# The first expert layer of a four-layer decoder: rows turned two tiles ahead, its weights on another queue, a small summary moved, and additions fixed behind their gathers

## The chip, the cores and the metric

The kernel runs on one core of a Trainium2 chip, as one program launched once. The metric is the device time of that core in microseconds (us), from the program's start to its end. Lower is better. The engines are named as in the profile: PE does matrix products, PEld is the loading of its weights (the operand that stays put), DVE is the vector engine, ACT the scalar engine (ScalarE), POOL is GpSimd, and SP issues most of the DMA transfers.

## The reference

Four decoder layers are applied to `x` (4 batches, 256 rows, 256 columns) with a context `ctx` (4, 1601, 256), all in fp32. Each layer is `x + attention(x, ctx)` and then `x + ffn(norm(x))`. Only parts of layers 0 to 2 matter here.

The feed-forward part of layer 0 is a mixture of 32 experts, of which each of the 1024 rows takes 8:

```
sel_w, sel_e = top_k(x @ gate_w.T, 8);  sel_w = softmax(sel_w)
g, u = x @ w_gate_proj[e].T, x @ w_up_proj[e].T          # I = 96
out = sum over the 8 chosen e of sel_w[e] * (silu(g) * u) @ w_down_proj[e].T
```

The attention of layer 1 reads the context through a decayed scan and then takes the mean of all its states, so that one vector per batch, the summary, is added to every row before a LayerNorm:

```
s[t] = K * s[t-1] + (ctx[t] @ W_in.T + b_in);  summary = mean over t of (s[t] @ W_out.T + b_out)
y = x + summary;  x = x + layernorm(y) * gamma + beta
```

The feed-forward part of layer 1 is a mixture of 8 experts with 2 chosen per row, and shared experts beside them. Layer 2 is attention with 4 key and value heads of 128 columns; its keys are normalised products of the context, `rms_norm(ctx @ wk_ctx)`, and its values are `ctx @ wv_ctx`. They depend on nothing that layers 0 and 1 compute.

## The kernel before, in words

**Layer 0's experts** (`l0_ffn`, from line 311) don't multiply every row by every expert. The 1024 x 8 pairs of row and expert are sorted by expert into NS = 95 tiles of 128 rows, each of a single expert. Eight DMAs, issued by SP (L338, L339), bring the weights, eight experts in each. `normed` (L105) normalises x, writes it to DRAM as `xd` from ScalarE's queue (L113) and turns it for the product with the router, whose logits are copied at L356. A long chain of small DVE steps (L356 to L378) finds the eight largest logits of each row and the place of each pair in the sorted order. To find the source row of each place, one-hot matrices are built by DVE (`cols` and `rows`, L385 to L389, of four groups of 128 rows at a time) and multiplied by PE (L397). The result is copied to `src`.

Then comes the loop of 95 tiles. POOL gathers 128 rows of `xd` by indirect DMA (L405, four buffers `f0xr`). `brought` turns them on PE (L444) and ScalarE copies the turned rows out of PSUM into `f0xsT` (L446, three buffers). `through` multiplies them by the gate and up weights of the tile's expert, which a register picks (`f0gu`), and ScalarE and DVE form silu(g) * u (L456, L457). `turned` turns that (L462, L464), `down` multiplies it by the down weights, DVE copies the result (L471) and SP writes it to `yd` in DRAM. The steps are staggered: in step s the order is `through(s)`, `brought(s + 1)`, `turned(s - 1)`, `down(s - 2)`.

**Adding back** (`l0_add`, L490). For each of 8 groups of 128 rows, POOL gathers eight results per row from `yd` (eight indirect DMAs, 64 in all). One group later DVE adds them with their gates to x (L510). Every second group, `l1_xattn` does the attention of layer 1 for one batch on DVE. When t is 1 the function `l1_summary` (L1115) computes the four summaries: two small products of `csum` with W_in (`mean`, L1125), four of the mean with W_out (`sm`, L1132). Its weights and vectors are loaded by `l1_open` (L1100). The loads of layer 1's expert weights (`l1_weights`, L630: eight DMAs) are issued from SP, one at each step of t.

**Layer 1's experts** (`l1_ffn`, L643) work in the same way with 23 tiles. Its tail (L836 to L847) gathers two results per row for eight groups and adds each right after the statement that gathers it.

**What fills PE.** `fill(n)` (L98) takes n steps of `l2_early` (L1147), which prepares layer 2's keys and values for 15 pairs of batch and head. One pair takes 7 product steps (8 passes of 256 columns, two ScalarE copies to `kr_early` and `va_early`, L1177 and L1178, and a write of the values by SP, L1179; `va_early` has four buffers), a norm, and 4 turning steps (L1202, a ScalarE copy, L1204, and a write, L1205). The list F0 says how many steps go where in the routing of layer 0 (8 after the logits, 10 in `slots`, 8 before each half of the one-hot products, 4 before the loop), G0 = 9 how many follow each group of `l0_add`, and F1 those of layer 1. What is left is done in layer 2's attention. The context of the next batch (`ctxT`) is loaded when a batch's first pair begins.

**What sets the order.** The program is written in the order of the work, and a planner in the framework orders each engine's instructions from it: among those that are ready by its own estimates, the one that stands earlier in the program goes first. `pin` (L96) forces an instruction to stay behind the one that was traced before it on the same engine. Each engine then works strictly through its list, and an instruction that waits holds all behind it. DMAs of SP and ScalarE wait in these lists too.

Of the kernel before, what the change touches and what calls it, by code (L numbers as in the profile page):

```python
# [11 lines left out]
F32 = mybir.dt.float32  # L12
BF16 = mybir.dt.bfloat16
U8 = mybir.dt.uint8
F16 = mybir.dt.float16
# [3 lines left out]
ALU = mybir.AluOpType  # L19
# [5 lines left out]
B = 4  # L25
# [20 lines left out]
F0 = [0, 0, 0, 0, 8, 10, 8, 4]  # L46
G0 = 9
REGS = 4
F1 = [1, 2, 2, 3, 0, 24]
# [8 lines left out]
class Kernel:  # L58
# [254 lines left out]
    def l0_ffn(self, one):  # L313
# [17 lines left out]
        with ExitStack() as es:  # L331
            wp = es.enter_context(tc.tile_pool(name="f0w", bufs=1))
            rt = es.enter_context(tc.tile_pool(name="f0r", bufs=1))
            two = es.enter_context(tc.tile_pool(name="f0two", bufs=2))
            w13 = wp.tile([P, E0, 2, 2 * I0], F32, name="f0w13")
            w2 = wp.tile([I0, E0, D], F32, name="f0w2")
            for e in range(0, E0, 8):
                nc.sync.dma_start(w13[:, e : e + 8], self.i["l0_w13"][:, e : e + 8])  # L338
                nc.sync.dma_start(w2[:, e : e + 8], self.i["l0_w2"][:, e : e + 8])  # L339
# [14 lines left out]
            self.fill(F0[B])  # L354
            l = rt.tile([P, 8, E0], F32, name="l0_l")
# [45 lines left out]
            nc.vector.tensor_copy(src, st[:, :NS])  # L401
            xr = []
# [38 lines left out]
            def brought(n):  # L441
                tp = ps.tile([P, 2, P], F32, name="f0tpx", tag="tp")
                for k in range(2):
                    nc.tensor.transpose(tp[:, k, :], xr[n][:, k * P : (k + 1) * P], self.ident)  # L444
                t = two.tile([P, 2, P], F32, name="f0xsT", bufs=3)
                nc.scalar.copy(t, tp)  # L446
# [183 lines left out]
    def l1_weights(self, pool):  # L630

        w = self.w1f = []
        for n, shape, parts in (
            ("l1_s13", [P, 2, 2, 2 * I1], 1), ("l1_s2", [P, 3, D], 1), ("l1_w13", [P, E1, 2, 2 * I1], 4),
            ("l1_w2", [H1, E1, 2, D], 2),
        ):
            w.append(pool.tile(shape, F32, name=n))
            c = shape[1] // parts
            for e in range(0, shape[1], c):
                self.pin(self.nc.sync.dma_start(w[-1][:, e : e + c], self.i[n][:, e : e + c]))  # L640
                yield

    def l1_ffn(self):  # L643
# [11 lines left out]
        with ExitStack() as es:  # L655
# [3 lines left out]
            s13, s2, w13, w2 = self.w1f  # L659
            xd = self.dram.tile([NT, D], F32, name="f1xd")  # L660
# [176 lines left out]
            for t in range(8):  # L837
                for r in range(K1):
                    yt = two.tile([P, D], F32, name="f1yt", bufs=6)
# [4 lines left out]
                    xt = self.x[t // 2][:, t % 2, :]  # L844
                    nc.vector.scalar_tensor_tensor(xt, yt, gate[:, r, t : t + 1], xt, ALU.mult, ALU.add)
                self.fill(F1[B + 1] // 8)
# [253 lines left out]
    def l1_open(self, es):  # L1100
        nc, i = self.nc, self.i
        one = self.a1 = es.enter_context(self.tc.tile_pool(name="a1", bufs=1))
# [5 lines left out]
        nc.sync.dma_start(b_in, i["l1_bin"].rearrange("(k p) -> p k", p=P))  # L1108
        rows = self.rows1 = {}
        for n in ("l1_bout", "l1_gamma", "l1_beta"):  # L1110
            rows[n] = one.tile([P, D], F32, name=n)
            nc.sync.dma_start(rows[n], i[n].to_broadcast([P, D]))
        self.w1 = (*w, b_in)

    def l1_summary(self):  # L1115

        nc, one = self.nc, self.a1
        w_in, w_out, b_in = self.w1
        nc.vector.tensor_scalar(b_in, b_in, self.swb, None, ALU.mult)
        mean = one.tile([P, 2, B], F32, name="mean")  # L1120
# [5 lines left out]
        self.summary = []  # L1126
        for b in range(B):
# [3 lines left out]
            sm = one.tile([P, D], F32, name=f"sm1{b}")  # L1131
            nc.vector.tensor_tensor(sm, sp, self.rows1["l1_bout"], ALU.add)  # L1132
            self.summary.append(sm)
# [12 lines left out]
    def l2_early(self, ctxT):  # L1146
# [17 lines left out]
        def products(u):  # L1164
# [3 lines left out]
            for m in range(0, NM, 2):  # L1168
# [7 lines left out]
                va = e2.tile([P, 2, HD2], F32, name="va_early", bufs=4)  # L1176
# [857 lines left out]
    def run(self):  # L2034
# [7 lines left out]
        with ExitStack() as es1:  # L2042
# [4 lines left out]
            one = es1.enter_context(tc.tile_pool(name="f0one", bufs=1))  # L2047
            self.l0_ffn(one)
            weights = self.l1_weights(es1.enter_context(tc.tile_pool(name="f1w", bufs=1)))
            with ExitStack() as es:  # L2050
                self.l1_open(es)
                self.l0_add(self.a1, weights)
            self.l1_ffn()
# [136 lines left out]
```

## Time and profile before

| | us |
|---|---|
| three runs | 2672.34, 2672.18, 2665.82 |
| median | 2672.18 |
| the profiled execution's own time | 2689.12 |
| span in its profile | 2687.4 |
| busy in the span: PE, PEld | 2503.5, 1507.0 |
| busy in the span: DVE, ACT, POOL | 1464.8, 1315.8, 751.5 |
| layer 0's attention ends | 141 |
| routing of layer 0 | 141 to 226 |
| loop of 95 tiles | 231 to 398 |
| `l0_add` | 398 to 524 |
| routing of layer 1, its loop, its tail | 524 to 612, to 670, to 702 |

A row of "costliest groups" names the line, engine, operation and tiles, the busy time and the mean of one in ns, and then the idle time of the engine just before it with what ended it. "PE MATMUL fill" at L74 are the products of `l2_early`, since L74 is the line of the helper that issues all products. In the answer on waits, a line gives the engine, the instruction that waited and what for, the total in us, how often, and the longest. In an answer in order of time, the first column is the start in us, the second the length, and `x4` that four instructions of one kind are put together. The 40 slices are 67.2 us each.

### The profile page before, as it was taken

To read this page: it belongs to the slowest core of one execution; us is meant where nothing else is said; L and a number is where in the kernel's file an instruction comes from. 1 tells how busy PE (TensorE), PEld (TensorE's weight loads), DVE (VectorE), ACT (ScalarE), POOL (GpSimd) and SP (SyncE) were. 2 spreads that over 40 slices of the span, in tenths; PEclk is the share of its full clock that TensorE was granted. 3 is DMA by queue.
4 is the path that set the end of the run, shared out by engine and by line. 5 is a ranking of instruction groups with operands and counts; after the bars stand their busy time and mean duration, and the time that the engine had idled before them with its cause. 6 is when DMAs were issued, how large, how long until landed. Compare 5 with 4: busy or idle time off the path is not lost. (4 is left out here: it accounts for less than half of the span.)

```text
span 2687.4 us, 47127 instructions
## 1 busy us (share of the span) xinstructions
PE 2503.5 (93%) x17800; PEld 1507.0 (56%) x17816; DVE 1464.8 (55%) x3031; ACT 1315.8 (49%) x2959; POOL 751.5 (28%) x1038
## 2 busy tenths in 40 slices
PE   7979994899689999999999999998998999999997
PEld 4667773677545555555555555655554554545553
DVE  6343534743467777777777777675234314233323
ACT  2334442452454445444444444442325775757775
POOL 1014546202334433433444444332101102001000
PEclk8989997899899999999999999999999999999998
DMA  5154575633621111111111110003212100000000
GB/s 199 57 194 137 161 149 155 210 98 89 196 95 45 41 38 46 45 46 45 45 45 45 45 43 28 9 9 133 90 72 73 33 2 27 4 3 2 5 6 5
DMA packets 93631, 186.24 MB, mean 69 GB/s; under 512 B 14924, under 2 KB 62736, under 8 KB 91312
## 3 DMA queue, kind: packets, MB, share of 16 engines
q1 hardware_dynamic: 79142, 150.80, 16.7%
q0 software_dynamic: 10416, 28.46, 4.7%
q10 hardware_dynamic: 3850, 3.97, 0.5%
q8 instruction: 145, 2.38, 0.4%
q14 instruction: 78, 0.64, 0.1%
HBM read 136.77 MB, written 46.42 MB: 68 GB/s over the span
## 5 line engine op out<-in xcount | busy, mean ns | idle before, releaser
L1448 ACT ACTIVATE p<-s,nm 128x448 f32<-128x448 f32 (+1 forms) x512 | 326.5, 644 | 424.3 <-DVE nm L1444 263.7
L1909 ACT ACTIVATE e<-s 128x1024 f32<-128x1024 f32 (+1 forms) x448 | 404.3, 960 | 158.7 <-PE s L74 153.9
L74 PE MATMUL s<-kT,qT 128*32 128x448 f32 (+1 forms) x4096 | 470.2, 556 | 10.0 <-ACT p L1448 5.0
L74 PE MATMUL o<-pT,va 128*128 128x256 f32 (+2 forms) x1920 | 431.1, 376 | 6.0 <-DVE pT L1490 6.0
L1484 POOL TENSOR_SCALAR p<-p,rm 128x448 f32<-128x448 f32 (+1 forms) x512 | 322.5, 652 | 370.0 <-DVE rm L1477 339.7
L74 PEld LDWEIGHTS o<-pT,va 128*128 128x128 f32 (+1 forms) x1920 | 344.4, 191 | 93.1 <-issue 51.4
L1490 DVE STREAM_TRANSPOSE pT<-p 128x896 f32<-128x896 f32 (+1 forms) x256 | 283.9, 1128 | 36.7 <-POOL p L1484 33.1
L1444 DVE TENSOR_REDUCE nm<-s 128x2 f32<-128x896 f32 (+1 forms) x256 | 282.7, 1105 | 3.4
L74 PE MATMUL s<-qb,kT 32*128 32x256 f32 (+1 forms) x3328 | 267.9, 404 | 13.2 <-ACT e L1909 11.0
L74 PEld LDWEIGHTS s<-kT,qT 128*32 128x32 f32 x4096 | 123.6, 109 | 264.9 <-issue 222.5
L74 PE MATMUL o<-e,va 128*32 128x256 f32 (+1 forms) x3328 | 235.7, 391 | 1.3 <-DVE os L2006 1.3
L74 PEld LDWEIGHTS s<-qb,kT 32*128 32x128 f32 (+1 forms) x3328 | 162.9, 181 | 105.2 <-issue 75.4
L74 PE MATMUL fill<-wkc_early,ctxT 128*128 128x256 f32 x780 | 184.6, 396 | 30.4 <-ACT va_early L1178 19.3
L74 PEld LDWEIGHTS fill<-wkc_early,ctxT 128*128 128x128 f32 x780 | 151.5, 197 | 59.6 <-ACT va_early L1178 21.9
L74 PEld LDWEIGHTS o<-e,va 128*32 128x32 f32 (+1 forms) x3328 | 90.6, 110 | 114.9 <-issue 74.9
L1936 POOL TENSOR_TENSOR x<-x,t 128x32 f32<-128x32 f32 x64 | 14.7, 250 | 438.7 <-DVE t L1931 438.7
L1441 DVE TENSOR_TENSOR s<-s,mask 128x128 f32<-128x128 f32 (+1 forms) x256 | 83.2, 325 | 67.3 <-PE s L74 62.3
L405 POOL DMA_INDIRECT f0xr<-f0xd,f0src x95 | 90.8, 956 | 80.6 <-PE f0tph L462 64.6
L1336 POOL TENSOR_TENSOR qo<-qo,qt 128x512 f32<-128x512 f32 x32 | 40.7, 1272 | 242.0 <-DVE rm L1477 139.6
L1448 ACT ACTIVATION_READ_ACCUMULATOR p<-s,nm 128x1 f32 x512 | 101.8, 199 | 0.0
L74 PE MATMUL f0gu<-f0w,f0xsT 128*128 x380 | 87.4, 353 | 1.4 <-ACT f0xsT L446 1.2
L1177 ACT COPY kr_early<-fill 128x256 f32<-128x256 f32 (+1 forms) x105 | 37.4, 356 | 101.3 <-PE fill L74 90.6
(510 smaller groups left out, 3494.2 us busy)
## 6 DMA issues: line engine op xcount, KB each, us to landing
ctxT<-in_ctxT SPq DMA_DIRECT2D x10, 1664.0 KB
f0yd<-f0ys SPq DMA_DIRECT2D x95, 128.0 KB
vd<-va_early SPq DMA_DIRECT2D x90, 128.0 KB
kd<-kT_early SPq DMA_DIRECT2D x45, 256.0 KB
kT<-kd SPq DMA_DIRECT2D x15, 768.0 KB
va<-vd SPq DMA_DIRECT2D x15, 768.0 KB
wq<-in_l_wq SPq DMA_DIRECT2D x16, 512.0 KB
wo<-in_l_wo SPq DMA_DIRECT2D x16, 512.0 KB
```

Of the source, the lines that this page charges most:

```text
L74: self.nc.tensor.matmul(out, lhsT, rhs, start=start, stop=stop, **kw)
L405: nc.gpsimd.indirect_dma_start(out=t, out_offset=None, in_=xd[:, :], in_offset=bass.IndirectOffsetOnAxis(ap=src[:, n : n + 1], axis=0),)
L1177: nc.scalar.copy(kr[:rows, m : m + n, :], tp[:rows, :n, :HD2])
L1336: nc.gpsimd.tensor_tensor(o1, o1, t2, ALU.add)
L1441: nc.vector.tensor_tensor(sv, sv, mask[:, 2 * c : 2 * c + 2, : nt - CT, :].rearrange("p n t i -> p n (t i)"), ALU.add)
L1444: nc.vector.tensor_reduce(nm[:, 2 * c : 2 * c + 2], s[:, :, : nt * 32], AX.X, ALU.max, negate=True)
L1448: nc.scalar.activation(p[:, n, : nt * 32], s[:, n, : nt * 32], AF.Exp, bias=nm[:, e : e + 1], accum_out=sm[:, e : e + 1],)
L1484: nc.gpsimd.tensor_scalar(p[:, n, : nt * 32], p[:, n, : nt * 32], r[:, e : e + 1], 1.0, ALU.mult, ALU.mult)
L1490: nc.vector.transpose(pT[:, 2 * c : 2 * c + 2, :nt, :].rearrange("p n t i -> p n (t i)"), p[:, :, : nt * 32])
L1909: nc.scalar.activation(e[:kr, :, :n, :], s[t][:kr, :, :n, :], AF.Exp, scale=1.0 / math.sqrt(HD3))
L1936: nc.gpsimd.tensor_tensor(xt, xt, t[:, q], ALU.add)
```

## The change

The change does the following.

1. The weights of layer 0's experts are issued by ScalarE in 16 DMAs of four experts each, instead of by SP in eight of eight experts.
2. F0 is 6, 8, 4, 4 instead of 8, 10, 8, 4. The one-hots are built in four parts of two groups, not two of four, so that 4 fill steps stand before each of four parts. They have a pool of their own, closed before the loop's buffers are opened.
3. `l1_summary` is called in `l0_ffn`, after the logits and the fill that follows them. Its loads (`l1_load`) are issued before `l0_ffn` starts; gamma and beta stay in `l1_open`.
4. Rows are brought two tiles ahead of their products: `brought(0)` and `brought(1)` stand ahead of the loop, and step s calls `brought(s + 2)`. `f0xsT` has four buffers.
5. In `l0_add` the additions are pinned, so that DVE keeps them in the order of the program. The loads of layer 1's expert weights begin at t = 6, so that three are issued there; the other five are issued at the start of `l1_ffn`.
6. In layer 1's tail the additions are done two groups after their gathers and are pinned; `f1yt` has `3 * K1` buffers, the same six. Three fill steps follow each of ten passes (30) instead of each of eight (24).
7. `va_early` has six buffers instead of four.

The core of the diff:

```diff
-F0 = [0, 0, 0, 0, 8, 10, 8, 4]
+F0 = [0, 0, 0, 0, 6, 8, 4, 4]
-F1 = [1, 2, 2, 3, 0, 24]
+F1 = [1, 2, 2, 3]
+G1 = 3
...
-            for e in range(0, E0, 8):
-                nc.sync.dma_start(w13[:, e : e + 8], self.i["l0_w13"][:, e : e + 8])
-                nc.sync.dma_start(w2[:, e : e + 8], self.i["l0_w2"][:, e : e + 8])
+            for e in range(0, E0, 4):
+                nc.scalar.dma_start(w13[:, e : e + 4], self.i["l0_w13"][:, e : e + 4])
+                nc.scalar.dma_start(w2[:, e : e + 4], self.i["l0_w2"][:, e : e + 4])
...
             self.fill(F0[B])
+            self.l1_summary()
...
-            for half in range(2):
+            hot = es.enter_context(ExitStack())
+            oh2 = hot.enter_context(tc.tile_pool(name="f0oh", bufs=2))
+            for part in range(4):
                 ones = []
-                for t in range(4 * half, 4 * half + 4):
-                    cols = two.tile([P, NS, K0], F16, name="f0cols", bufs=4)
-                    rows = two.tile([P, P, K0], F16, name="f0rows", bufs=4)
+                for t in range(2 * part, 2 * part + 2):
+                    cols = oh2.tile([P, NS, K0], F16, name="f0cols")
+                    rows = oh2.tile([P, P, K0], F16, name="f0rows")
...
-                t = two.tile([P, 2, P], F32, name="f0xsT", bufs=3)
+                t = two.tile([P, 2, P], F32, name="f0xsT", bufs=4)
...
             brought(0)
+            brought(1)
             for s in range(NS + 2):
                 if s < NS:
                     hs[s] = through(s)
-                    if s + 1 < NS:
-                        brought(s + 1)
+                    if s + 2 < NS:
+                        brought(s + 2)
...
-            if t == 1:
-                self.l1_summary()
             if t:
                 xt = self.x[(t - 1) // 2][:, (t - 1) % 2, :]
                 for r in range(K0):
-                    nc.vector.scalar_tensor_tensor(xt, rows.pop(0), gate[:, t - 1, r : r + 1], xt, ALU.mult, ALU.add)
+                    self.pin(
+                        nc.vector.scalar_tensor_tensor(xt, rows.pop(0), gate[:, t - 1, r : r + 1], xt, ALU.mult, ALU.add)
+                    )
...
             self.fill(G0)
-            next(weights, None)
+            if t > 5:
+                next(weights, None)
...
+            for _ in weights:
+                pass
...
-            for t in range(8):
-                for r in range(K1):
-                    yt = two.tile([P, D], F32, name="f1yt", bufs=6)
+            rows = []
+            for t in range(10):
+                for r in range(K1 if t < 8 else 0):
+                    yt = two.tile([P, D], F32, name="f1yt", bufs=3 * K1)
...
+                    rows.append(yt)
+                if t > 1:
+                    xt = self.x[(t - 2) // 2][:, (t - 2) % 2, :]
+                    for r in range(K1):
+                        self.pin(
+                            nc.vector.scalar_tensor_tensor(
+                                xt, rows.pop(0), gate[:, r, t - 2 : t - 1], xt, ALU.mult, ALU.add
+                            )
+                        )
-                self.fill(F1[B + 1] // 8)
+                self.fill(G1)
...
-                va = e2.tile([P, 2, HD2], F32, name="va_early", bufs=4)
+                va = e2.tile([P, 2, HD2], F32, name="va_early", bufs=6)
...
+            self.l1_load(one)
             self.l0_ffn(one)
```

More of the change, by code (lines that the diff above doesn't have):

```diff
@@ L333, in l0_ffn @@
             rt = es.enter_context(tc.tile_pool(name="f0r", bufs=1))
-            two = es.enter_context(tc.tile_pool(name="f0two", bufs=2))
             w13 = wp.tile([P, E0, 2, 2 * I0], F32, name="f0w13")
             w2 = wp.tile([I0, E0, D], F32, name="f0w2")
-            for e in range(0, E0, 8):
-                nc.sync.dma_start(w13[:, e : e + 8], self.i["l0_w13"][:, e : e + 8])
-                nc.sync.dma_start(w2[:, e : e + 8], self.i["l0_w2"][:, e : e + 8])
+            for e in range(0, E0, 4):
+                nc.scalar.dma_start(w13[:, e : e + 4], self.i["l0_w13"][:, e : e + 4])
+                nc.scalar.dma_start(w2[:, e : e + 4], self.i["l0_w2"][:, e : e + 4])
             src = rt.tile([P, NS], U32, name="f0src")
@@ L401, in l0_ffn @@
             nc.vector.tensor_copy(src, st[:, :NS])
+            hot.close()
+            two = es.enter_context(tc.tile_pool(name="f0two", bufs=2))
             xr = []
@@ L630, in l1_weights, with l1_ffn @@
     def l1_weights(self, pool):
-        w = self.w1f = []
-        for n, shape, parts in (
+        sizes = (
             ("l1_s13", [P, 2, 2, 2 * I1], 1), ("l1_s2", [P, 3, D], 1), ("l1_w13", [P, E1, 2, 2 * I1], 4),
             ("l1_w2", [H1, E1, 2, D], 2),
-        ):
-            w.append(pool.tile(shape, F32, name=n))
+        )
+        self.w1f = [pool.tile(shape, F32, name=n) for n, shape, _ in sizes]
+        yield
+        for w, (n, shape, parts) in zip(self.w1f, sizes):
             c = shape[1] // parts
             for e in range(0, shape[1], c):
-                self.pin(self.nc.sync.dma_start(w[-1][:, e : e + c], self.i[n][:, e : e + c]))
+                self.pin(self.nc.sync.dma_start(w[:, e : e + c], self.i[n][:, e : e + c]))
                 yield
-    def l1_ffn(self):
+    def l1_ffn(self, weights):
         nc, tc = self.nc, self.tc
@@ L843, in l1_ffn @@
                     )
-                    xt = self.x[t // 2][:, t % 2, :]
-                    nc.vector.scalar_tensor_tensor(xt, yt, gate[:, r, t : t + 1], xt, ALU.mult, ALU.add)
-                self.fill(F1[B + 1] // 8)
+                    rows.append(yt)
[6 more added lines that the diff above has]
+                            )
+                        )
+                self.fill(G1)
             self.scaler = nc.gpsimd
@@ L1097, in l2_add, with l1_load @@
             )
-    def l1_open(self, es):
+    def l1_load(self, one):
         nc, i = self.nc, self.i
-        one = self.a1 = es.enter_context(self.tc.tile_pool(name="a1", bufs=1))
         w = []
@@ L1108, in l1_open @@
         nc.sync.dma_start(b_in, i["l1_bin"].rearrange("(k p) -> p k", p=P))
+        b_out = one.tile([P, D], F32, name="b_out")
+        nc.sync.dma_start(b_out, i["l1_bout"].to_broadcast([P, D]))
+        self.w1 = (*w, b_in, b_out)
+        self.summary = [one.tile([P, D], F32, name=f"sm1{b}") for b in range(B)]
+        self.mean1 = one.tile([P, 2, B], F32, name="mean")
+    def l1_open(self, es):
+        nc, i = self.nc, self.i
+        one = self.a1 = es.enter_context(self.tc.tile_pool(name="a1", bufs=1))
         rows = self.rows1 = {}
-        for n in ("l1_bout", "l1_gamma", "l1_beta"):
+        for n in ("l1_gamma", "l1_beta"):
             rows[n] = one.tile([P, D], F32, name=n)
             nc.sync.dma_start(rows[n], i[n].to_broadcast([P, D]))
-        self.w1 = (*w, b_in)
     def l1_summary(self):
-        nc, one = self.nc, self.a1
-        w_in, w_out, b_in = self.w1
+        nc = self.nc
+        w_in, w_out, b_in, b_out = self.w1
         nc.vector.tensor_scalar(b_in, b_in, self.swb, None, ALU.mult)
-        mean = one.tile([P, 2, B], F32, name="mean")
+        mean = self.mean1
         for h in range(2):
@@ L1125, in l1_summary @@
             nc.vector.tensor_scalar(mean[:, h, :], ms, b_in[:, h : h + 1], 1.0 / M, ALU.add, ALU.mult)
-        self.summary = []
         for b in range(B):
@@ L1130, in l1_summary @@
                 self.mm(sp, mean[:, h, b : b + 1].to_broadcast([P, P]), w_out[:, h, :], h == 0, h == 1)
-            sm = one.tile([P, D], F32, name=f"sm1{b}")
-            nc.vector.tensor_tensor(sm, sp, self.rows1["l1_bout"], ALU.add)
-            self.summary.append(sm)
+            nc.vector.tensor_tensor(self.summary[b], sp, b_out, ALU.add)
     def l1_xattn(self, b):
@@ L2047, in run @@
             one = es1.enter_context(tc.tile_pool(name="f0one", bufs=1))
+            self.l1_load(one)
             self.l0_ffn(one)
             weights = self.l1_weights(es1.enter_context(tc.tile_pool(name="f1w", bufs=1)))
+            next(weights)
             with ExitStack() as es:
@@ L2052, in run @@
                 self.l0_add(self.a1, weights)
-            self.l1_ffn()
+            self.l1_ffn(weights)
         self.l2_xattn()
```

## The prediction

> **What bounds the kernel now.** I read the 40 slices first, then the busy time by stretches, then the waits and the order of time inside the stretches that are not full.
>
> ```profile
> PE   7979994899689999999999999998998999999997
> PEclk8989997899899999999999999999999999999998
> 135.00:160.00 25.00, 22.48 (x128) 19.92 (x127) 11.44 (x49) 7.98 (x18) 2.65 (x10) 1.00 0.75 253
> 160.00:200.00 40.00, 24.46 (x109) 20.34 (x110) 15.24 (x46) 16.36 (x40) 6.99 (x9) 0.79 0.52 165
> 200.00:250.00 50.00, 44.36 (x221) 35.97 (x220) 16.61 (x34) 20.05 (x57) 20.18 (x21) 0.90 0.40 128
> 250.00:400.00 150.00, 149.39 (x804) 111.97 (x803) 68.31 (x202) 69.87 (x266) 79.26 (x84) 1.00 0.65 155
> 400.00:450.00 50.00, 22.17 (x84) 15.98 (x83) 14.63 (x37) 9.55 (x23) 30.42 (x33) 0.66 0.49 148
> 450.00:524.00 74.00, 57.27 (x244) 45.38 (x242) 55.20 (x148) 32.55 (x90) 34.07 (x36) 0.88 0.63 199
> 524.00:612.00 88.00, 85.95 (x440) 68.62 (x439) 39.07 (x145) 47.21 (x121) 10.40 (x28) 1.00 0.37 114
> ```
>
> A row of the second kind is a stretch, its length, then busy time (and count) of PE, PEld, DVE, ACT and POOL, the granted clock, the DMA share, GB/s. From about 700 us on PE is full and the change touches nothing there. It acts between 141 and 702 us, where PE is lacking in two places: 160 to 200 (15.5 us idle) and 400 to 524 (44.6 us). PE is the bound elsewhere. In 250 to 400, the loop of 95 sorted tiles, PE looks full, yet its weight side waits:
>
> ```profile
> PEld f0gu L74 <- ACT f0xsT L446: 31.8, 85, 0.4
> 301.53 0.62 PEld L74 LDWEIGHTS f0gu<-f0w,f0xsT 128*128 128x128 f32 x4 [0.38 <-ACT f0xsT L446]
> 303.18 0.62 PEld L74 LDWEIGHTS f0gu<-f0w,f0xsT 128*128 128x128 f32 x4 [0.38 <-ACT f0xsT L446]
> L405 POOL DMA_INDIRECT f0xr<-f0xd,f0src x95 | 90.8, 956 | 80.6 <-PE f0tph L462 64.6
> ```
>
> One tile takes 303.18 - 301.53 = 1.65 us, and in it the first weight load stands 0.38 us for ScalarE's copy of the turned rows. POOL, with 0.956 us a gather, is idle half of the time. The first hole comes from writes:
>
> ```profile
> PE fill L74 <- ACT va_early L1178: 17.1, 1, 17.1
> SPq L1179 <- DMA f0xd<-xn: 12.0, 1, 12.0
> SPq L339 <- DMA f0w<-in_l_w: 3.3, 1, 3.3
> ```
>
> PE stands 17.1 us for a copy to a value tile (va_early) whose four buffers are all waiting to be written out; SP holds those writes behind the eight weight loads. The second hole, in order of time:
>
> ```profile
> 412.11 1.16 PE L74 MATMUL fill<-csum,l_win 128*128 128x4 f32 x8 [2.89 <-ACT va_early L1178]
> 421.05 1.22 PE L74 MATMUL fill<-l_wout,mean 128*128 128x256 f32 x2 [7.78 <-issue]
> 434.96 2.07 PE L74 MATMUL fill<-l_wout,mean 128*128 128x256 f32 x4 [7.80 <-issue]
> 443.39 2.07 PE L74 MATMUL fill<-l_wout,mean 128*128 128x256 f32 x4 [6.35 <-DVE sm L1132]
> ```
>
> These few matmuls of the mean summary are some 9 us of work spread over 409 to 445 us while POOL gathers; fills queue behind them.
>
> **What the Trainium skill says.** "DMA: Bandwidth & Descriptors", section "Issuing engines are not separate DMA queues": loads issued by another engine run on the same 16 DMA engines and save sequencer time only. The trace agrees that the transfer is the limit: the 9.4 MB of weights, landing in 146 to 171, keep the share at 0.93 to 1.00 and move 293 to 349 GB/s. The same page, "Queues, rings and completion order": SP's and ScalarE's queues are separate rows which each engine serves in turn. So the value writes need no longer follow all weights; no run here shows both rows loaded. "TensorE: Matmul & The Clock Gate", section "What's actually happening": an idle PE is granted half the clock. The trace agrees: 0.54 in 410 to 447 us.
>
> **The change, part by part**, against the profiled execution (2689.1 us, span 2687.4). That one lies 16.9 us above the median 2672.2 of the three runs; I carry differences over unchanged.
>
> *Weights by ScalarE (141 to 200).* Bytes are the same, 9.4 MB or about 30 us at 310 GB/s. Issues go from 8 to 16; SP's rows took 0.34 to 0.55 us each, so ScalarE spends 16 x 0.42 = 6.7 us issuing. Good side: value writes bypass the weights, and six buffers instead of four hold two products' time more, so the 17.1 us go. Bad side: in before SP's last weight issue already waited 3.3 us for an earlier weight load. If every issue past the eighth waits likewise, ScalarE stands until eight of 16 loads have landed, some 4.7 MB at 310 GB/s = 15 us. Queued behind it are the xnT copies, ln_rs and the fills' copies; PE and the routing chain wait for those. Then PE's hole only moves from 157 to 142. Gain: 0 to 17; I take 6.
>
> *Fill steps.* F0 goes from 8+10+2x8+4 = 38 to 6+8+4x4+4 = 34. A unit of 11 steps is about 12.9 us of PE, 1.17 a step: 4.7 us gained here. Four parts of one-hots (2 x 1.65 us on DVE from the rows 0.55, 0.69, 0.41 us) hide beneath their 4 steps = 4.7 us; without this cover, 3.3 us each for the last two parts. The 4 steps reappear later; G0 stays 81, the tail of layer 1 gets 30 for 24, and layer 2 is left with 2 fewer: 2.3 us gained. The six extra in the tail cost nothing if PE is idle there (612 to 701: 71.8 of 89 busy), 7 us if not. I take 0.
>
> *Summary in the routing chain.* 24 small matmuls and 7 DVE steps, about 5 us of PE work and 2.5 of DVE. DVE's routing steps end at 171.5 and their product is first wanted by PE at 203.2, so DVE has some 30 us to spare. I take +3, bounds 0 and +31 (if hand-offs are as slow here as in 412 to 443). Four moved loads (0.5 MB) cost 2 us of DMA, before the routing starts.
>
> *ctxT load.* It is issued at 230.2 now, 1.66 MB, while the first gathers run; 231 to 240 us shows PE 3.4 of 9 us busy at a DMA share of 0.95. With four steps fewer the load falls past the loop. Up to 5 us gained, some given back at the gathers after it: I take 2.
>
> *Rows two tiles ahead.* The copy is then done a tile early, so the 0.38 us wait goes. Not all of it counts: PE's array is still busy with the down product during part of it. By the starts of its passes a tile without a wait is 4 x 0.163 (gate/up) + 2 x 0.11 + 0.107 (turns) + 2 x 0.215 (down) = 1.41 us, 0.25 less than 1.65. Next limits: POOL at 0.956 plus 0.30 between gathers = 1.26; ScalarE 0.25 + 0.37 + 0.26 = 0.88; DVE 0.67; DMA share 0.65 x 1.65/1.41 = 0.76. None reaches 1.41, POOL comes near. 95 x 0.25 = 24 us gained; bounds 13 and 34 (0.14 and 0.36 a tile).
>
> *l0_add (398 to 524).* The summary leaves, so fills stay in PE's stream during the first gathers; five of the eight weight loads of layer 1 leave too and three come late. POOL's 64 gathers need 64 x 1.26 = 81 us and took 97.3 (402.6 to 499.9). 81 fill steps are 95 us of PE; only 49 were through at 524, the rest ran in the routing of layer 1. The floor is 44.6 us of PE idle removed. But part of that hole belongs to the gathers' tail (a fill's transposes wait for ScalarE copies 6 to 7 us late at 462 to 475 too), and nothing in the change makes that faster. Pinned additions stand in DVE's order ahead of the fills' scales and the next norm: if a gather is late, these are late as well, and PE's fills behind them. Gain 0 to 45; I take 20.
>
> *Layer-1 weights.* Five of eight loads, 5 x 704 KB = 3.5 MB or 12 us at 300 GB/s, are now issued together at the start of l1_ffn, ahead of the fills' writes on SP. They land before the loop at 612. Fills may stall like those at 157, less what six buffers hold: 0 to 12 us; I take +4.
>
> *Tail of layer 1.* 16 gathers x 1.25 = 20 us pace it as before; additions two tiles late add nothing. 0, bounds -5 and +5.
>
> Sum: -6 - 4.7 - 2.3 + 3 - 2 - 24 - 20 + 4 + 0 = -52 us. Profiled 2637; median 2672 - 52 = 2620, 1.9% faster.
>
> **The rivals.**
> *The loop finds another limit*: the planner keeps the turns where they were, or POOL's gathers and the random 1 KB rows set the pace near 1.6 us. For: 1.26 us is only 0.15 below 1.41, and copies of down products already waited 12.4 us for write-outs near the loop's end. Against: POOL's idle time of 80.6 us. The loop then gains 5: 2620 + 19 = 2639.
> *l0_add keeps its time*: the late hand-offs come from gathering itself and pinned additions repeat them. For: 462 to 475. Against: fills at 402 to 409 run at full speed beside gathers. 2620 + 20 = 2640.
> *Everything goes well*: stall 17, l0_add 40, loop 26 gained, nothing lost at layer 1 or to the summary: another 40 us, 2580.
> *Slower*: ScalarE is held by its own weight issues for the whole transfer. With value writes taking half of the DMA, 9.4 MB at 150 GB/s is 63 us. From the end of this hold on the chain needs 8.7 us (turn, copy, logits: 141.4 to 150.1), 21.4 (DVE), 22.7 (203.2 to 225.9, first to last one-hot product) and 5 (gather, first turn): 58 us, so the loop starts at 141 + 63 + 58 = 262, not 231: +31. A hold of 32 us starts the loop where it starts now. With the loop's 13 at the low end, nothing from l0_add, 4 lost at layer 1 and 2 gained in layer 2: 31 - 13 + 4 - 2 = +20: 2692. It decides from a hold of 32 + 11 = 43 us. Against it: only the first eight of the sixteen loads must have landed before the last is issued.
>
> **How the numbers follow.** Forecast 0.44, 2605 to 2632; loop limit 0.15; l0_add unchanged 0.20; all well 0.12; slower 0.09. A measurement tells 0.3%, 8 us, from no change. Faster: 0.44 + 0.12 + 0.20 + 0.15, less 0.05 for two of these rivals together with the small costs at their high ends: 0.86; same 0.05; slower 0.09. The range leaves out the slower rival and about half of the good one: 2583 to 2667.
>
> **What would show it.** Right: the f0xsT wait gone and gate/up loads 1.4 us apart; no fill wait on va_early of over 5 us near 157; no summary lines after 400; PE over 80% busy in l0_add. Wrong: ScalarE's DMA issues with waits between 142 and 158 and xnT copies behind them; summary lines stretched over 30 us in the routing; a tile still at 1.6 us; PE idle beside the gathers as now; fills waiting on va_early after l1_ffn's start.

## The result, and the profile after

The changed kernel takes 2637.6 us (median of 4 runs, 2635.6 to 2638.5) against 2669.9 for the kernel before (4 runs, 2665.8 to 2672.3). The ratio is 0.9879, with a 95% interval of 0.9862 to 0.9897: 32 us or 1.2% less. The forecast was 2620, 52 us less, in a band of 2605 to 2632 that 2637.6 overshoots. The changed kernel's profiled execution took 2638.45 us with a span of 2636.7, so between the two *profiles* the span fell by 50.7 us. The difference between 50.7 and 32 is the first thing to explain: the profiled execution of before, from which every term was taken, was 17 us slower than the other runs of before, while that of after is not.

The rows of the changed kernel that answer to those of before. First the 40 slices, then busy time by stretches (length; PE, PEld, DVE, ACT, POOL; clock; DMA share; GB/s):

```profile
PE   7989988898799999999999999998998999999997
PEclk8989999999999999999999999998999999999998
```

```profile
135.00:160.00 25.00, 13.32 (x73) 11.79 (x71) 4.07 (x13) 3.27 (x8) 2.66 (x10) 0.78 0.78 265
160.00:200.00 40.00, 38.85 (x171) 31.88 (x172) 25.91 (x87) 16.88 (x41) 6.37 (x7) 0.84 0.43 148
250.00:400.00 150.00, 140.12 (x817) 123.15 (x816) 73.25 (x210) 72.31 (x271) 90.21 (x107) 0.98 0.75 181
400.00:450.00 50.00, 43.95 (x205) 35.15 (x204) 36.59 (x82) 27.72 (x75) 34.01 (x38) 0.97 0.66 197
450.00:524.00 74.00, 62.36 (x289) 50.14 (x287) 51.67 (x131) 35.43 (x95) 18.25 (x20) 0.93 0.71 230
```

The hole of 160 to 200 is closed, but one has opened in 135 to 160. In 400 to 450 PE is busy for 44 us where it was 22. The loop, in order of time on the weight side:

```profile
302.26 0.73 PEld L75 LDWEIGHTS f0gu<-f0w,f0xsT 128*128 128x128 f32 x4
303.67 0.73 PEld L75 LDWEIGHTS f0gu<-f0w,f0xsT 128*128 128x128 f32 x4
```

No wait stands behind these rows any more, and a tile takes 303.67 - 302.26 = 1.41 us. POOL is idle before its gathers (now L410) for 51.3 us instead of 80.6.

```profile
L410 POOL DMA_INDIRECT f0xr<-f0xd,f0src x95 | 92.3, 972 | 51.3 <-PE f0tph L467 43.2
```

The longest wait of PE in 141 to 231 us, and then the only rows of the mean summary. They now stand in the routing of layer 0, within 5.5 us, with four short products of the routing between the first row and the second and no idle time:

```profile
PE f0gu L75 <- ACT xnT L72: 11.7, 1, 11.7
```

```profile
173.48 0.51 PE L75 MATMUL fill<-csum,l_win 128*128 128x4 f32 x4
174.79 0.51 PE L75 MATMUL fill<-csum,l_win 128*128 128x4 f32 x4
175.15 3.87 PE L75 MATMUL fill<-l_wout,mean 128*128 128x256 f32 x16
```

To see where the time went, the span is cut at five events that every kernel has, read from the views in order of time: the first gate/up product of the loop, the last down product, the first and last products of layer 1's loop, and the last product of a fill with the context (called the last fill; it falls in layer 2's attention). Lengths in us:

| | before, first profile | before, second | changed | changed, again |
|---|---|---|---|---|
| start to the loop | 232.8 | 233.1 | 231.0 | 233.0 |
| loop of 95 tiles | 164.8 | 165.0 | 146.2 | 146.8 |
| its end to layer 1's loop (l0_add, routing) | 214.9 | 200.2 | 188.8 | 189.0 |
| layer 1's loop | 57.6 | 57.7 | 57.7 | 57.6 |
| its end to the last fill (tail and start of layer 2) | 63.5 | 54.6 | 55.1 | 54.2 |
| rest | 1953.8 | 1955.5 | 1957.9 | 1959.0 |
| span | 2687.4 | 2666.1 | 2636.7 | 2639.6 |

The second profile of before and the repeat of the changed kernel are experiments told below. Up to the last fill, 31.8 us separate the second column from the third: 2.1 before the loop, 18.8 in it, 11.4 behind it, and 0.5 lost in the tail. The rest is 2.4 us longer, which is less than its spread over the profiles of before (1953.8 to 1960.2, with a third one below).

### The profile page after: what moved, and what is told of

It is laid out like the page before. It is cut to its first block, busy times and chain, and to the rows that moved or that the text cites. A ratio compares the mean times of both kernels' runs of the same rounds, so it can differ in the third digit from the quotient of the medians.

```text
span 2636.7 us, 47077 instructions
## 1 busy us (share of the span) xinstructions
PE 2491.9 (95%) x17816; PEld 1517.6 (58%) x17816; DVE 1480.0 (56%) x3039; ACT 1310.9 (50%) x2957; POOL 750.8 (28%) x1030
## 5 line engine op out<-in xcount | busy, mean ns | idle before, releaser
L1959 POOL TENSOR_TENSOR x<-x,t 128x32 f32<-128x32 f32 x64 | 14.7, 252 | 439.7 <-DVE t L1954 439.7
L410 POOL DMA_INDIRECT f0xr<-f0xd,f0src x95 | 92.3, 972 | 51.3 <-PE f0tph L467 43.2
L75 PE MATMUL f2gu<-f2wgu,f2xsT 128*128 x176 | 84.3, 603 | 0.6 <-ACT f2xsT L72 0.3
```

Source lines behind the costliest of these rows:

```text
L75: self.nc.tensor.matmul(out, lhsT, rhs, start=start, stop=stop, **kw)
L410: nc.gpsimd.indirect_dma_start(out=t, out_offset=None, in_=xd[:, :], in_offset=bass.IndirectOffsetOnAxis(ap=src[:, n : n + 1], axis=0),)
L1959: nc.gpsimd.tensor_tensor(xt, xt, t[:, q], ALU.add)
```

## The experiments

After the result my theory was: the loop and the emptier l0_add are real gains, ScalarE's queue has moved the first hole and not removed it, and some 17 us of the holes in the first profile are not typical. The rival: the profile of before is right, and the changed kernel has a cost that its profile doesn't show.

The runs stood in three sets of four, each set on one chip and each timed beside the kernel before there: 2670.1, 2694.4 and 2672.9 us. On the second set's chip this kernel was slower, so the four runs there are compared with each other, by stretches, and not with those of the other sets.

**Before, once more** (no edit).

> The kernel before, unchanged, profiled once more. Theory A (the profiled execution of before was not typical: it took 2689 us where the other runs took 2666 to 2672, and the surplus sits in the hole beside the gathers, 400 to 450 us): this profile's own time is 2665 to 2675, PE's busy time in 400 to 450 us is 32 or more instead of 22, and the matmuls of the mean summary lie closer together than 412 to 445. Theory B (profiling always slows this kernel, or the surplus is spread over the whole span): own time near 2689 again, the hole as before, or the difference in no single stretch.

Measured: ratio 0.9998 (0.9988 to 1.0008), profiled span 2666.1. The summary's rows in this profile:

```profile
412.90 1.55 PE L74 MATMUL fill<-csum,l_win 128*128 128x4 f32 x8 [3.17 <-ACT va_early L1178]
422.75 5.77 PE L74 MATMUL fill<-l_wout,mean 128*128 128x256 f32 x16 [8.30 <-DVE mean L1125]
```

In the first profile the sixteen products with W_out came in groups of 2, 6, 4 and 4 with gaps of up to 8 us, from 421 to 445; here they run in one piece, after one gap of 8.3. PE's busy time in 400 to 450 is 33.5 us instead of 22.2. The table shows where the first profile was longer: 14.7 us behind the loop, 8.9 in layer 1's tail, nowhere else. In both, POOL gathers while PE's fills come in short bursts. Theory A holds, though 8.9 us of the surplus lie in the tail, which it had not named.

**Two tiles ahead alone.** Before, with the fourth `f0xsT` buffer, the one-hots in four parts so that the buffers fit, and

```diff
+            brought(1)
...
-                    if s + 1 < NS:
-                        brought(s + 1)
+                    if s + 2 < NS:
+                        brought(s + 2)
```

> Before with the rows turned two tiles ahead and the fourth f0xsT buffer alone; the one-hots get the pool of their own in four parts, since the buffers don't fit otherwise, and the number of fill steps stays 38. Theory A (the loop alone gives what its stretch of the changed kernel shows, 18 to 19 us, and nothing later takes it back, since PE bounds what follows): 2669 - 18 = 2651, ratio 0.993. Rival (the results of the loop only reach the gathers of l0_add earlier, which write-outs of the last tiles hold back, so that part is lost): 2660, ratio 0.9965 or nearer to 1.

Measured: 0.9937 (0.9924 to 0.9950), 2654.6 us, 15.5 us less. The loop takes 147.5 us (234.9 to 382.4), 17.5 less than before's second profile, and starts 1.8 later. All stretches behind it together are 2.6 us longer, which is within the spread of the rest. So the loop's gain arrives at the end almost whole: half of the change's gain comes from this part.

**Weights by SP again.** The changed kernel, with

```diff
-            for e in range(0, E0, 4):
-                nc.scalar.dma_start(w13[:, e : e + 4], self.i["l0_w13"][:, e : e + 4])
-                nc.scalar.dma_start(w2[:, e : e + 4], self.i["l0_w2"][:, e : e + 4])
+            for e in range(0, E0, 8):
+                nc.sync.dma_start(w13[:, e : e + 8], self.i["l0_w13"][:, e : e + 8])
+                nc.sync.dma_start(w2[:, e : e + 8], self.i["l0_w2"][:, e : e + 8])
```

> The changed kernel with the eight weight DMAs of layer 0 on SP again, all else as changed. Theory A (ScalarE's queue only moves PE's hole from 157 to 146 us; with six value buffers the old hole is some 10 us shorter than 17): 11.7 us of PE idle at 146 to 157 goes, 5 to 8 us at the writes of values comes: 2634, ratio to before 0.987, between 0.985 and 0.989. Rival B (ScalarE's queue is worth its hold, because the value writes pass the weights): the 17 us hole is back in full, 2643 or more, ratio 0.990 or above.

Measured: 0.9847 (0.9832 to 0.9862), 2628.2 us: about 8 us *faster* than the changed kernel (0.9847 against 0.9879 and 0.9875). Neither number was met; the sign is theory A's, the size is larger. The wait of 11.7 us is gone and one of 10.6 for a value buffer (PE for va_early; 5 to 8 expected) has come, yet the loop starts at 225.9 and not at 231.0, and the stretch behind the loop is 4.4 us shorter. One reason can be read in the rows of time. In the changed kernel the hole lies ahead of the routing: DVE copies the logits at 166.4 us, with the weights on SP at 150.6, while SP's hole lies beside DVE's routing steps. PE also comes out of the changed kernel's hole at a granted clock of 0.50 (157 to 161 us), so that 16 small router products take 3.62 us where 16 took 1.87 before. The shorter stretches behind the loop are not explained. This edit changes the queue and the number of DMAs together; the next one parts them.

**Eight weight DMAs, still from ScalarE.** The same edit with `nc.scalar` kept.

> The changed kernel with the weights on ScalarE's queue in eight DMAs of eight experts, not sixteen of four. Theory A (ScalarE stands because each DMA past the eighth waits until the one eight places earlier has landed): with eight there is almost nothing to wait for, the 18.1 us before the xnT copy shrinks to under 8, and PE's hole of 11.7 us at 146 goes; value writes may then stand for a landing and take 0 to 8 us back: 2632, ratio 0.986, between 0.984 and 0.989. Rival B (the hold comes from the bytes in flight, not from the number of DMAs): ScalarE still stands 15 to 18 us, same time as the changed kernel, 2637, ratio 0.988.

Measured: 0.9832 (0.9817 to 0.9847), 2623.5 us, 12 us faster than the changed kernel. ScalarE's list around the weights, first in the changed kernel, then here (ACTq rows are DMA issues):

```profile
143.81 0.44 ACTq L338 DMA_DIRECT2D f0w<-in_l_w  x1
144.29 0.47 ACTq L339 DMA_DIRECT2D f0w<-in_l_w  x1
145.52 0.34 ACTq L338 DMA_DIRECT2D f0w<-in_l_w  x1
...
155.53 0.34 ACTq L338 DMA_DIRECT2D f0w<-in_l_w  x1
156.59 0.33 ACTq L339 DMA_DIRECT2D f0w<-in_l_w  x1
156.97 0.59 ACT L72 COPY xnT<-tp_ln 128x512 f32<-128x512 f32 x1 [18.13 <-DMA f0w<-in_l_w]
```

```profile
144.38 0.44 ACTq L338 DMA_DIRECT2D f0w<-in_l_w  x1
144.86 0.46 ACTq L339 DMA_DIRECT2D f0w<-in_l_w  x1
145.36 0.58 ACT L72 COPY xnT<-tp_ln 128x512 f32<-128x512 f32 x1 [5.89 <-PE fill L75]
```

The first eight issues follow each other at 0.5 us in both. From the ninth on each comes with a landing, one or two us apart, and the copy that PE needs stands behind the sixteenth, 11.6 us later than with eight. That is theory A: the number of DMAs holds ScalarE, not the bytes. With eight DMAs the queue itself is worth little: from SP the kernel takes 2628.2 us, from ScalarE 2623.5, and the two intervals overlap.

The value writes did not get past the weights by being on another queue. Here SP still waits for weight landings before it issues them:

```profile
SPq L1202 <- DMA f0w<-in_l_w: 40.8, 7, 15.2
```

The first wait (15.2) reaches back to a time before there was a value to write. After it the second and third write are issued at 156.5 and 159.9 us, though ScalarE has had these values ready since 148.6 and 155.2. So the eight look like a count that SP and ScalarE share. PE's waits for va_early come to only 2.2 us, so six buffers cover it.

**The summary back in l0_add** (only the call; its loads stay early).

```diff
-            self.l1_summary()
...
+            if t == 1:
+                self.l1_summary()
```

> The changed kernel with the call of the summary at t = 1 of l0_add again (its loads stay early). Theory A (the hole beside the first gathers comes from the summary's short hand-offs between engines): PE waits for mean or sm again in 385 to 420 us, 8 to 20 us in sum, and only 3 to 5 us come back in the routing of layer 0: 2637 + 9 = 2646, ratio to before 0.991. Rival B (the hole comes from the two late loads and the gathers, the summary only stands in it): 2637 or up to 3 us either way, ratio 0.987 to 0.989.

**Layer 1's weights spread.**

```diff
-            if t > 5:
-                next(weights, None)
+            next(weights, None)
```

> The changed kernel with layer 1's eight weight loads issued one at each step of l0_add, as before, and none left for the start of l1_ffn. Theory A (five loads together hold back the writes of normed rows, so that DVE stands 10.7 us for them and PE 5.8): these waits go, 4 us less: 2633, ratio 0.986. Rival B (loads beside gathers cost the gathers as much or more): 2637 to 2645, ratio 0.988 to 0.991.

**The tail of before**: gather and addition in one step, not pinned, three fill steps in each of eight passes.

```diff
-            for t in range(10):
-                for r in range(K1 if t < 8 else 0):
+            for t in range(8):
+                for r in range(K1):
...
-                if t > 1:
-                    xt = self.x[(t - 2) // 2][:, (t - 2) % 2, :]
+                    xt = self.x[t // 2][:, t % 2, :]
+                    nc.vector.scalar_tensor_tensor(xt, yt, gate[:, r, t : t + 1], xt, ALU.mult, ALU.add)
...
                 self.fill(G1)
```

> The changed kernel with layer 1's tail as before: each addition right after its gather, not pinned, eight passes, three fill steps in each (24, not 30). Theory A (from the last product of layer 1's loop to the last fill the changed kernel takes 55.1 us against 54.6 before, so the new tail is worth nothing): 2635 to 2640, ratio 0.987 to 0.989. Rival B (the new tail gains something that the stretches don't show, since its fills come earlier): 2643 or more, ratio 0.990.

**Additions of l0_add not pinned.**

```diff
-                    self.pin(
-                        nc.vector.scalar_tensor_tensor(xt, rows.pop(0), gate[:, t - 1, r : r + 1], xt, ALU.mult, ALU.add)
-                    )
+                    nc.vector.scalar_tensor_tensor(xt, rows.pop(0), gate[:, t - 1, r : r + 1], xt, ALU.mult, ALU.add)
```

> The changed kernel with the additions of l0_add not pinned. Theory A (the pins keep fill work and its scales ahead of the next additions as in the program, so that PE is fed beside the gathers; without them the planner moves additions and PE waits as before): l0_add's fills thin out, PE idle in 380 to 524 us rises by 8 us or more, 2645, ratio 0.991. Rival B (pins do nothing to the sum; what the fills lose in l0_add they take in the routing of layer 1): within 3 us of the changed kernel, ratio 0.987 to 0.989.

These four form the second set. Ratios to before there: 0.9969 (0.9957 to 0.9982), 0.9947 (0.9934 to 0.9960), 0.9993 (0.9984 to 1.0001), 0.9953 (0.9941 to 0.9966). The expectations in ratios missed, all but the open-ended rival B of the tail, most likely because the changed kernel itself gains less on that chip. It was not run there, so that is open. The stretches can be compared, and the kernel with the old tail has the program of the changed one up to the end of layer 1's loop. Each column is one profile, so differences of a few us carry little weight:

| us | summary back | weights spread | tail of before | no pins |
|---|---|---|---|---|
| start to the loop | 230.5 | 235.1 | 233.6 | 230.8 |
| loop | 156.0 | 156.0 | 155.3 | 155.3 |
| loop's end to layer 1's loop | 230.9 | 214.5 | 222.1 | 216.5 |
| its end to the last fill | 55.8 | 54.6 | 66.6 | 59.6 |
| median of the runs | 2687.0 | 2680.7 | 2694.2 | 2683.0 |

*Summary*: its return costs 8.8 us beside the gathers (230.9 against 222.1) and frees 3.1 ahead of the loop, 6 us in all. That speaks for theory A, with a smaller size. PE's only wait for the mean or its sums that the profile names there is

```profile
PE fill L75 <- DVE mean L1152: 4.7, 1, 4.7
```

*Weights spread*: DVE's wait for the written normed rows, 10.1 us in the old-tail kernel and 10.7 in the changed one, is not in this kernel's list, and PE's of 4.6 is gone: theory A's mechanism. The stretch is 7.6 us shorter, but PE has two new waits, 10.7 us in sum, that the profile puts down to "remote", a releaser it can't name, and the median less the tail is 2626.1 us against 2627.6 with the old tail. So a gain in the total is not shown.

*Tail*: rival B, in direction. Up to the last fill the old tail is 7 to 12 us longer than the three others. Part of that is not lost: with six more steps left to layer 2, the last fill stands behind more of layer 2's own products (26, against 21, 7 and 21), and the rest of the span is 2 to 7 us shorter (1951.8 us against 1954.1 to 1958.8). Tail and rest together are 2 to 9 us longer. In the first and third sets before and after take the same 54 to 55 us, with 38 steps of fill left in before and 42 in the changed kernel. My theory, nothing, had compared unequal work.

*Pins*: not decided. Without them the gathers end 18 us sooner (489.4 against 507.2) and the stretch is 5.6 us shorter, not longer, but PE stands 24.8 us in three waits put down to "remote", and 4 to 5 us come back in the tail. No gain of the pins is visible here.

*The loop there*: in all four kernels every third tile is late. In the fifth to the 78th spacing, 23 or 24 of 74 are over 1.6 us, nearly all of them three apart, where the changed kernel has 2. `f0ys` has three buffers, so results that land later on that chip would show like this; five buffers were not run there.

**The changed kernel again** (no edit).

> The changed kernel, unchanged, once more. Theory A (the gain depends on the chip: where gathers and their signals are slower and before takes 2690 us or more, the loop gains 9 to 10 us instead of 18.8 and the fills beside the gathers gain little): where before takes 2670 the ratio is 0.988 again; where it takes 2690 or more it is 0.994 to 0.997. Rival B (the gain is the same everywhere, and the four kernels of the second set lose what their edits lost): ratio 0.987 to 0.990 on either kind.

Measured: 0.9875 (0.9857 to 0.9894), 2640.4 us beside 2672.9: the first branch of theory A and also B's number, since before is quick on this chip. It doesn't tell them apart. It does confirm the changed kernel's profile to 3 us of span.

**Five result buffers in the loop.**

```diff
-                ys = two.tile([P, D], F32, name="f0ys", bufs=3)
+                ys = two.tile([P, D], F32, name="f0ys", bufs=5)
```

> The changed kernel with five buffers of results (f0ys) in the loop instead of three. Theory A (what keeps the loop from its 24 us is that DVE stands some 25 us for write-outs of results, in 18 cases, and PE behind it): the waits of f0ys for f0yd fall below 8 us, the loop is 3 to 6 us shorter, ratio to before 0.002 lower than that of the changed kernel in this set. Rival B (the DMA engines are full then, so that more buffers only move the wait): the loop as in the changed kernel within 1.5 us.

Measured: 0.9868 (0.9850 to 0.9885), 2636.8 us; the interval holds the changed kernel's ratio. The wait of f0ys for its write-outs, in the changed kernel

```profile
DVE f0ys L476 <- DMA f0yd<-f0ys: 25.4, 19, 4.2
```

has left the list, and the loop takes 145.4 us instead of 146.8. Rival B: the wait was a symptom. What is behind it shows in the stretches of the changed kernel's loop:

```profile
300.00:330.00 30.00, 30.00 (x193) 28.36 (x192) 16.72 (x49) 15.86 (x63) 20.72 (x22) 1.00 0.71 188
350.00:365.00 15.00, 11.83 (x65) 9.05 (x65) 4.18 (x16) 5.82 (x23) 7.57 (x8) 1.00 0.98 137
```

At 350 the DMA engines are busy 98% of the time while they move less. The queue of the gathers in these two stretches:

```profile
q0 software_dynamic: 1020, 2.80, 43.8%
```

```profile
q0 software_dynamic: 368, 1.00, 76.9%
```

It needs 0.438 x 30 / 2.80 = 4.7 us of all engines for a MB at first, and 0.769 x 15 / 1.00 = 11.5 later; a gather lands after 7.2 us instead of 3.7. From the fifth tile on, tiles start 1.41 us apart up to the 79th, with two exceptions, then 1.2 to 3.4. Counting the experts' rows from the reference's inputs, the sum of ceil(count / 128) is 78: the last 17 tiles hold nobody's rows, and their places all point to row 0. The queue of the write-outs takes 2.9 us a MB in both stretches, so it is the gathers that are dear. That reading one row 128 times is what slows these gathers is likely, but no run here tried it.

**Both: eight weight DMAs and five result buffers.**

> The changed kernel with both: eight weight DMAs instead of sixteen on ScalarE's queue, and five result buffers. Theory A (the two hold PE at different times, so their gains add): 0.0047 of ratio for the eight, as in the first set, and 0.002 for the buffers, 0.006 to 0.007 below the changed kernel in this set, 16 to 18 us. Rival B (the earlier loop runs into other waits): 0.003 or less below it.

Measured: 0.9813 (0.9798 to 0.9829), 2623.2 us, 17 us (0.65%) faster than the changed kernel in the same set and 1.9% faster than before. It is theory A's number. The five buffers alone had 0.0007 of ratio, within the noise, so the eight DMAs carry it.

**Before, a third profile** (no edit).

> The kernel before, a third profile, to set its stretches beside those of the changed kernel on one chip. Theory A (the first profile of before was taken where gathers and signals are slow): if the other runs of before are near 2670 here, the stretch from the last result of the loop to the first product of layer 1's loop takes 200 us as in the second profile; if they are at 2690 or more, 215 us as in the first. The loop takes 165 us in either. Rival B: the stretch varies from run to run on one chip, whatever the times.

Measured: span 2671.3, other runs 2672.9. The stretch behind the loop is 198.9 us, the tail 55.4, the loop 163.6, the rest 1960.2. So two profiles of before agree and the first stands apart in two stretches. Which condition made it so isn't settled. It looks like the second set, where before takes 2694, but no profile of before was taken there.

## Why the prediction came out as it did

The direction was right, and so were the mechanisms of the loop and of the summary. What failed as a mechanism is the good side of the weights, that value writes would pass them. The size, 52 us against 32, was too large in every row, most of all in the loop. By its steps, against the second profile of before:

| step | forecast | measured |
|---|---|---|
| up to the loop: weights -6, four steps -4.7, summary +3 | -7.7 | -2.1 |
| loop -24, ctxT -2 | -26 | -18.8 |
| l0_add -20, layer 1's weights +4 | -16 | -11.4 |
| tail and fills left for layer 2 | -2.3 | +0.5 |
| sum up to the last fill | -52 | -31.8 |

*"I carry differences over unchanged."* The forecast noted that the profiled execution lay 16.9 us above the median, and then took its holes for typical. The 44.6 us of idle PE in 400 to 524, from which the 20 were taken, are 30.0 in the second profile and 30.6 in the third. Against the first profile the stretches give -1.8, -18.6, -26.1 and -8.4, or 54.9 us. That this comes near 52 is luck: the first two rows had been put too high by 13 us, the last two too low by 16. The surplus of that execution wasn't spread over the span. It sat in l0_add and in the tail, and was no part of the runs that are compared.

*Weights by ScalarE.* Both sides had been priced, 0 or 17 us, and 6 was taken as a middle. The bad side came as described: 18.1 us from the last work to the xnT copy, forecast 15 for the wait, and PE's hole moved from 157 to 146, 11.7 us instead of 17.1. The reason given for the good side failed: SP's value writes still waited for weight landings, as the run with eight DMAs shows. The signs of being wrong that the forecast named, DMA issues with waits in 142 to 158 and the xnT copy behind them, are both there. There was no reason for a middle, because the trace of before already had the sign of it, SP's eighth issue waiting 3.3 us for an earlier landing.

*The summary in the routing.* Forecast +3; its return frees 3.1 us ahead of the loop in the second set.

*Rows two tiles ahead.* The period was right to 0.01 us, and the wait is gone. The term failed in its count: 95 tiles at 0.25 us less, 24 us, where the kernel with this part alone gained 17.5. Only the tiles up to the 79th run at 1.41; the last sixteen spacings, 28.3 us before, take 32.0, while the gathers there need 2.5 times the DMA time a MB. The first profile showed it: in before the last nine spacings are 1.65 to 2.08 us, and I had put the 12.4 us of waits for write-outs there down to the write-outs.

*ctxT.* It is issued at 379.7 instead of 230.2, and PE's busy time in 231 to 240 rises from 3.4 to 8.3 us. Not all of that is the load: with two tiles ahead alone it is still issued at 229.8, and there the first ten spacings take 17.9 us against 14.4 in the changed kernel, but the last sixteen 29.8 against 32.0. The whole loop differs by 1.3 us, so nothing shows that the 2 net were wrong.

*l0_add.* The fills' return was read rightly, PE is 88% and 84% busy in 400 to 450 and 450 to 524. The summary's stay beside gathers costs 6 us in the second set, of the 20 taken for all of it. The other large change is in PE's waits for value copies behind the loop. The second profile of before, then the changed kernel:

```profile
PE fill L74 <- ACT va_early L1178: 13.2, 6, 4.2
```

```profile
PE fill L75 <- ACT va_early L1201: 2.2, 3, 0.7
```

Six value buffers could do this, or the weight loads that left l0_add. Neither was taken back alone on a chip where the waits are gone, so this share is open; the forecast had given the buffers nothing here.

*Layer 1's weights.* Forecast +4 with a stall of values. PE's wait is 5.8 us in one place (3.9 in the repeat), behind DVE's 10.7 for the writes of normed rows. The size was about right, the thing that waits was another.

*Tail.* Four more steps of fill than before (6 here, 2 fewer in layer 2) run in the same 55 us. I had counted the two as a gain and the six as free. One profile each can't resolve such amounts: the rest of the span alone varies by more.

The rival *l0_add keeps its time* came nearest with 2640, but its reason isn't what was found: l0_add did gain, and the loop gained less.

## What to carry to other kernels

Where the profiled execution lies clear of the other runs, take a second profile before pricing its holes, and look in which stretch the two differ. A queue of DMAs on a computing engine was cheap here up to eight in flight, and from the ninth on it put that engine's real work behind landings: use fewer, larger transfers. Another engine's queue did not get the value writes past these loads either. And a period read from the middle of a loop holds for the tiles that look like those in the middle; look at the last ones before multiplying.

## What the runs showed of the hardware

- Sixteen DMAs from one engine: eight issues at 0.5 us each, then one per landing. Eight of twice the size moved the engine's next work from 157.0 to 145.4 us. With those eight out, value writes of the other queue (SP) stood 25.6 us in six waits for their landings, after a first one of 15.2 that began before there was a value to write.
- Gathers of 128 rows landed in 3.7 us for filled tiles and in 7.2 for tiles without rows of their own, at 4.7 and 11.5 us of all DMA engines a MB.
- The same kernel took 2670, 2673 and 2694 us on three chips. On the slowest, the loop of the four changed kernels took 155 to 156 us, where the changed kernel took 146 and 147 elsewhere, though the DMA time of its gathers was no higher (33.9% of 30 us for 2.50 MB, 4.1 us a MB, in the kernel with the old tail). What is slower there is open; every third tile was late.
